# An attention layer and a quantised FFN on one core: P @ latents, the output products and the weight loads moved by some steps

## The chip, the core and the metric

The kernel runs on one core of a Trainium2 chip. The core has TensorE (PE; its weight loads are a row of their own, PEld), VectorE (DVE), ScalarE (ACT), GpSimd (POOL) and SyncE (SP), which issues all transfers of this kernel, one after the other. Each engine works its instructions off in the order of the program and waits for the others by semaphores. The metric is the device time of one launch in microseconds.

## The reference

The input has 8 sequences ("batches") of 512 tokens with 512 features, all in float32. The layer is attention with compressed keys and values, 16 heads, and then a gated FFN whose weights are rounded to 8-bit floats:

```
x = x + attention(layernorm(x))
x = x + ffn(layernorm(x))

attention:  q = rmsnorm(h @ wq_a.T) @ wq_b.T            16 heads, 128 + 64 rotary
            kv_c, k_pe = split(h @ wkv_a.T)             128 latents + 64 rotary
            k, v = split(rmsnorm(kv_c) @ wkv_b.T)       per head
            attn = softmax((q.k + rope(q_pe).rope(k_pe)) / sqrt(192))
            out = (attn @ v) @ wo.T
ffn:        silu(h @ fp8(gate) * gs) * (h @ fp8(up) * us) @ fp8(down) * ds
```

## The kernel before

The weights of a head are folded: `wq_b` with the key half of `wkv_b` into `wa`, the value half of `wkv_b` with `wo` into `wst`. So a head's scores are taken against the 128 latents themselves, and P @ V becomes P @ latents with the value weights applied later.

The attention part is a list of 512 steps, one for each batch, head and tile of 128 queries (`steps`). A step number is `at(b, h, t) = (b * 16 + h) * 4 + t`; within a batch the steps run from 0 to 63, four a head. Each step does the following (`scores`, L547 to L569, and the loop at L793 on):

- First the `rest` of the step before: on VectorE the reciprocal of the row sums (L566), the scaling of the row (L567) and a transpose by blocks of 32 (L167). After every second tile `send` (L172) has SyncE write the block to DRAM (`way`, L177) and read it back, four transfers, as the transposed probabilities `prT` (L179). The second needs the first to have landed.
- Then the scores of this step: TensorE (L555, L557), the row maximum on VectorE (L559, `nmax`), the exponential on ScalarE (L562).
- Then whatever was put into this step of `work`, in the order in which it was put there. `put(i, f)` is all the planning that there is: the numbers in these calls are written by hand, and the order of each engine follows from them, because the scheduler is set to take the program's own order.

What is put there, with the step in the batch at which head h's or group g's work stands (i is the last step of a group's last head, 16 g + 15):

- `project(b, h)` (L537): query projection to the latents, on TensorE, copied out by ScalarE as `qn`. Step 4 h - 3.
- `project_pe`: rotary part for two heads: `qpe` on TensorE, `rotate` on VectorE with a sum on GpSimd (`roped`, L414), `hi` on ScalarE, `lo` on VectorE.
- `attend(b, h)` (L572): P @ latents, eight matmuls (`av`), copied out as `o` by ScalarE. Step 4 h + 8, five steps behind the head's last scores.
- `sums` (L587): four additions on GpSimd over two heads' `o`.
- `output(b, g)` (L601): four heads' contribution to the output, as a product of 2 x 2 blocks with seven products in place of eight. `product` (L616) runs 4 matmuls for a block and then adds the sum in PSUM to a quarter of `x` (L627). The products share sums: four of them go into `u_ps`, one behind the other without clearing, and are read after each; `z_ps` and `v_ps` share a second buffer. So a product into `u` can begin only when VectorE has read `u` for the product before. Steps i + 7, 8, 12 and 15.
- `load_wst`, `load_x`: loads by SyncE of the folded weights and of the batch's input. The buffer of the input, `x`, takes the sum of the attention and is stored to DRAM (`x2`, L631) at the end of the batch, before the next batch's input is loaded into it.
- `round_piece` (L383): in batches 1 to 6, one piece of FFN weights every four steps: load (`raw`), `first` (two operations on VectorE and two on GpSimd, L71 to L77), `rest` (two on VectorE, L81 and L82), store (`done`).
- The next batch's latents, in pieces spread over the batch (`latents`): layer norm, transposes, projection with `wlr` (`project_x`), `norms` (a square root on ScalarE, which changes its function table and back), `scale` (L473, L476), `transpose_l` (L483, L484, TensorE) and `rotary`.

PSUM has six buffers for everything but the products (`ps_r`), taken in turn. The last batch has no latents to make; it loads FFN weights instead. The FFN follows, batch by batch.

Of the kernel before, what the change touches and what calls it, by code (L numbers as in the profile page):

```python
# [43 lines left out]
P = 128  # L44
# [42 lines left out]
class Layer:  # L87
# [182 lines left out]
    def attention(self):  # L270
        tc, nc, ins, wp, xp = self.tc, self.nc, self.ins, self.wp, self.xp
        with ExitStack() as ctx:
# [110 lines left out]
            def round_piece(w, i, half):  # L383

                n = self.size[w]
                cols = slice(half * H // 2, (half + 1) * H // 2)
                got = {}

                def load():
                    got["raw"] = fp.tile([P, H // 2], F32, tag="wo", name="raw")  # L390
                    nc.sync.dma_start(got["raw"], ins[w][i][:, cols])

                def first():
                    got["done"] = fp.tile([P, H // 2], F32R, tag="wo", name="done")
                    got["rest"] = round_e4m3fn(nc, got["done"], got["raw"], sp)

                def store():
                    nc.sync.dma_start(
                        self.scratch[w, i // n][:, i % n, cols].bitcast(F32), got["done"].bitcast(F32)
                    )  # L400

                return load, first, lambda: got["rest"](), store
# [184 lines left out]
            def sums(b, h):  # L587

                even, odd = (state["o", b, h - 1 + k].rearrange("p (u s) -> p u s", u=2) for k in range(2))
                s = hp.tile([P, 3, S // 2], F32, tag="sums", name="sums", bufs=2)
                s2, s3, s4 = (s[:, k, :] for k in range(3))
                nc.gpsimd.tensor_tensor(s3, even[:, 0], even[:, 1], ALU.subtract)
                nc.gpsimd.tensor_tensor(even[:, 1], even[:, 1], odd[:, 1], ALU.add)
                nc.gpsimd.tensor_tensor(s2, even[:, 1], even[:, 0], ALU.subtract)
                nc.gpsimd.tensor_tensor(s4, odd[:, 0], s2, ALU.subtract)
                del state["pe", b, h // 2]
                state["sums", b, h] = even[:, 0], even[:, 1], s2, s3, s4, odd[:, 0], odd[:, 1]

            def output(b, g):  # L601


                x = xs[b]
                ops = [state.pop(("sums", b, g * G + k)) for k in (1, 3)]
                for j in range(G):
                    del state["o", b, g * G + j]
                w = wst_s.pop((b, g))
                c11, c12, c21, c22 = (
                    x[:, 2 * t : 2 * t + 2, k * (H // 2) : (k + 1) * (H // 2)] for t in range(2) for k in range(2)  # L610
                )
                A11, S1, S2, S3, S4, A12, A22 = range(7)
                B11, B21, B22, T1, T2, T3, T4 = range(7)
                got = {}

                def product(name, left, right, c, last=True):  # L616
                    first = name not in got
                    if first:
                        tag = "u" if name == "u" else "v"
                        got[name] = ps_o.tile([P, 2, H // 2], F32, tag=tag, name=f"{name}_ps")  # L620
                    for t in range(2):
                        for p in range(2):
                            nc.tensor.matmul(  # L623
                                got[name][:, t, :], ops[p][left][:, t * P : (t + 1) * P], w[:, p, right, :],
                                start=first and t == 0 and p == 0, stop=last and t == 1 and p == 1, skip_group_check=True,
                            )
                    nc.vector.tensor_tensor(c, c, got[name], ALU.add)  # L627

                def store(t):
                    if g == NG - 1:  # L630
                        nc.sync.dma_start(self.x2[b][:, t : t + 2, :], x[:, t : t + 2, :])  # L631

                return [
                    lambda: (product("u", A11, B11, c11, False), product("z", A12, B21, c11)),
                    lambda: (product("u", S2, T2, c12, False), product("v", S1, T1, c22, False)),
                    lambda: (product("u", S3, T3, c22, False), product("v", S4, B22, c12)),
                    lambda: store(0),
                    lambda: product("u", A22, T4, c21),
                    lambda: store(2),
                ]  # L640
# [14 lines left out]
            def put_q(b, h):  # L655

                i = at(b, h)
                if h % 2 == 0:

                    def rotary_part():  # L660
                        for k, f in enumerate(project_pe(b, h // 2)):
                            put(i - 5 + k, f)

                    put(i - 6, rotary_part)
                put(i - 3, project, b, h)


            p0, state["latents", 0] = latents(0)
# [26 lines left out]


            for b, h in ((b, h) for b in range(B) for h in range(NH)):
                put(at(b, h, 3) + 5, attend, b, h)
            for b, h in ((b, h) for b in range(B) for h in range(NH)):
                if b or h:  # L700
                    put_q(b, h)
            for b, h in ((b, h) for b in range(B) for h in range(1, NH, 2)):
                i = at(b, h, 3)
                put(i + 6, sums, b, h)
                if h % G == G - 1:

                    def projected(b=b, g=h // G, i=i):

                        when = (7, 8, 18, 13, 19, 17) if (b, g) == (B - 1, NG - 2) else (7, 8, 12, 13, 15, 17)
                        for n, f in zip(when, output(b, g)):  # L710
                            put(i + n, f)

                    put(i + 6, projected)

            for h in range(NH):
                if h >= 2:
# [15 lines left out]
            for b in range(1, B):  # L732
                for g in range(NG):
                    for k, f in enumerate(load_wst(b, g)):
                        put(at(b, G * g + 3, 3) - 6 + 2 * k, f)
                for k, f in enumerate(load_x(xs, b, hidden(b), xp, "x")):
                    put(at(b, 4, 1) + k + k // 2, f)

            todo = [(w, i) for i in range(NI) for w in ("wg", "wu")] + [("wd", i) for i in range(NI)]
            for k, (w, i, half) in enumerate((w, i, half) for w, i in todo for half in range(2)):  # L740
                b, n = divmod(k, 12)
                for d, f in zip((-2, 0, 3, 4), round_piece(w, i, half)):
                    put(at(b + 1, n + 2, 1) + d, f)


# [8 lines left out]
            def put_latents(b):  # L754
# [6 lines left out]
                put(at(b - 1, 13), p["norms"])  # L761
                put(at(b - 1, 13, 1), p["norms_inverse"])
                for t in range(NT):
                    put(at(b - 1, 13, 1) + t // 2, p["scale"], t)
                    put(at(b - 1, 13, 3) + t // 2, p["transpose_l"], t)
                put(at(b - 1, 14, 1), p["rotary"])

            def put_ffn():
                stats, apply, transpose, self.y = self.ffn_normed(self.fx[0], sp, ps_r, hp)
# [10 lines left out]
                put(at(b - 1, 3), *((put_latents, b) if b < B else (put_ffn,)))  # L780
            for g in range(NG):
                put(at(B - 1, G * g + 3, 1), self.load_ffn, "wg", g, wp, f"wa{g}")
            put(at(B - 1, NH - 1, 3) + 3, self.load_ffn, "wu", 0, wp, "wst", 2)

            self.gates = {}
            put(
# [3 lines left out]

            with tc.manual_schedule():
                prT = block = rest = None
                for i in range(len(steps) + 18):  # L793
                    if rest:
                        rest()
                        rest = None
# [142 lines left out]
```

## Time and profile before

| | before |
|---|---|
| median of 3 runs | 2803.2 us (2802.39 to 2813.38) |
| the profiled execution | 2801.86 us |
| its span, first to last instruction | 2800.0 us |
| TensorE busy | 2728.4 us, 97% of the span |
| VectorE busy | 1887.1 us, 67% |
| ScalarE, GpSimd busy | 899.0 us, 604.1 us |
| scores of all 512 steps end | 2236.4 us after the span's start |
| one batch in the middle | about 277 us |

The page of a profile lists busy time by engine, the chain of work that ended last, and groups of instructions by line with the idle time of their engine just ahead of them. The timeline gives single instructions: start, duration, engine, line, operation, output and inputs, shape, how often in a row, and in brackets the engine's idle time before it and what ended it. Matmuls overlap, and their ends are modelled, so one of 512 columns is shown as 0.6 us and the next begins after 0.43; an fp32 matmul counts as two instructions. The granted clock of TensorE is a share of full speed.

### The profile page before, as it was taken

The numbers are of one execution on the slowest core, as the hardware profiler recorded it, in microseconds if no ns is written. First come the engines' busy times: TensorE is split into PE (matmuls) and PEld (weight loads), VectorE is DVE, ScalarE is ACT, GpSimd is POOL, SyncE is SP. The second block draws the span as 40 slices with busy tenths as digits, with TensorE's granted clock in tenths as the row PEclk, the third lists the DMA queues.
The fourth block names the chain that finished last, engine by engine and source line by source line (L and its number), as shares of the span: only waits on it lengthen the run. The fifth ranks groups of instructions, "written<-read, shape, count | busy, mean of one in ns | idle before, by whom it ended". The sixth has DMA issues, their size and how long they took to land.

```text
span 2800.0 us, 29251 instructions
## 1 busy us (share of the span) xinstructions
PE 2728.4 (97%) x9264; PEld 1717.8 (61%) x9264; DVE 1887.1 (67%) x3680; ACT 899.0 (32%) x1956; POOL 604.1 (22%) x629
## 2 busy tenths in 40 slices
PE   7999999999999999999999999999999999999999
PEld 4555555555555555555555555555555578888887
DVE  5766777777777777777777777777766733443332
ACT  3333333333333333333333333333232323322222
POOL 1222222212221222122212221222111122222222
PEclk9999999999999999999999999999999999999999
DMA  4654555455545554555455445654565552111110
GB/s 131 211 175 158 170 193 166 154 174 188 169 153 178 184 162 154 178 190 162 152 179 192 159 153 180 194 167 145 176 193 168 178 184 81 61 61 64 64 64 19
DMA packets 262377, 426.07 MB, mean 152 GB/s; under 512 B 29648, under 2 KB 192592, under 8 KB 260688
## 3 DMA queue, kind: packets, MB, share of 16 engines
q1 hardware_dynamic: 262224, 424.21, 47.0%
q8 instruction: 74, 1.21, 0.2%
q14 instruction: 79, 0.65, 0.1%
HBM read 248.99 MB, written 175.11 MB: 151 GB/s over the span
## 4 chain that ended last, share of the span: by engine, by line
PE 85%; DVE 7%; DMA 4%; SPq 1%; issue 1%; ACT 1%; POOL 0%; ACTq 0%; POOLq 0%; DVEq 0%
PE av L578 13%; PE sc L555 13%; PE qn_ps L543 10%; PE u_ps L623 7%; PE sc L557 7%; PE pu L261 6%; PE pd L864 6%; PE pg L261 6%; PE qpe_ps L511 5%; PE lr_ps L448 4%; PE v_ps L623 4%; DMA way<-block 2%; PE z_ps L623 2%; DVE pr L567 2%; DVE block L167 1%; DMA raw<-in_wu 1%
## 5 line engine op out<-in xcount | busy, mean ns | idle before, releaser
L562 ACT ACTIVATE pr<-sc,nmax 128x512 f32<-128x512 f32 x512 | 352.0, 687 | 1296.2 <-DVE nmax L559 1296.0
L557 PE MATMUL sc<-kpe,qpe 128*128 128x512 f32 x1024 | 525.8, 594 | 2.1 <-DVE qpe L531 2.1
L555 PE MATMUL sc<-lat,qn 128*128 128x512 f32 x1024 | 523.1, 592 | 0.0
L578 PE MATMUL av<-prT,kvt 128*128 128x512 f32 x1024 | 471.1, 603 | 28.9 <-DMA prT<-way 19.7
L559 DVE TENSOR_REDUCE nmax<-sc 128x1 f32<-128x512 f32 x512 | 339.0, 662 | 123.2 <-PE sc L557 123.0
L167 DVE STREAM_TRANSPOSE block<-pr 128x512 f32<-128x512 f32 x512 | 364.2, 711 | 21.9 <-DMA way<-block 4.2
L543 PE MATMUL qn_ps<-lat,wa 128*128 128x512 f32 x768 | 350.4, 592 | 0.0
L567 DVE TENSOR_SCALAR pr<-pr,rden 128x512 f32<-128x512 f32 x512 | 334.3, 653 | 18.0
L557 PEld LDWEIGHTS sc<-kpe,qpe 128*128 128x128 f32 x1024 | 194.4, 190 | 247.4 <-issue 242.3
L578 PEld LDWEIGHTS av<-prT,kvt 128*128 128x128 f32 x1024 | 196.2, 193 | 234.6 <-issue 215.0
L414 POOL TENSOR_TENSOR roped<-rope_own,rope_sw 128x512 f32<-128x512 f32 x72 | 91.4, 1270 | 995.2 <-DVE rden L566 896.4
L555 PEld LDWEIGHTS sc<-lat,qn 128*128 128x128 f32 x1024 | 188.9, 190 | 136.1 <-issue 114.3
L543 PEld LDWEIGHTS qn_ps<-lat,wa 128*128 128x128 f32 x768 | 145.3, 189 | 134.5 <-issue 123.0
L852 POOL TENSOR_TENSOR fl<-fuse,fh 128x512 fp32r<-128x512 f32 x96 | 126.6, 1319 | 382.1 <-ACT fh L851 382.1
L848 DVE SCALAR_TENSOR_TENSOR fuse<-pu,us,gate 128x512 f32<-128x512 f32 x96 | 72.0, 750 | 198.3 <-PE pu L261 194.8
L566 DVE RECIPROCAL rden<-den 128x1 f32<-128x1 f32 x512 | 81.6, 159 | 152.3 <-ACT pr L562 144.8
L76 POOL TENSOR_TENSOR q_r<-raw,q_m 128x256 f32<-128x256 f32 x72 | 67.5, 938 | 512.3 <-DVE q_m L74 512.3
L511 PE MATMUL qpe_ps<-lat,wqp 128*128 128x512 f32 x384 | 175.1, 592 | 0.0
L623 PE MATMUL u_ps<-wst,sums 128*128 128x256 f32 x512 | 126.3, 391 | 24.2 <-DVE x L627 16.2
L261 PE MATMUL pg<-yh,wg 128*128 128x512 f32 x384 | 149.6, 390 | 0.0
L261 PE MATMUL pu<-yh,wu 128*128 128x512 f32 x384 | 149.6, 390 | 0.0
L261 PE MATMUL pu<-yl,wu 128*128 128x512 f32 x384 | 149.4, 389 | 0.0
(115 smaller groups left out, 3719.3 us busy)
## 6 DMA issues: line engine op xcount, KB each, us to landing
way<-block SPq DMA_DIRECT2D x256, 512.0 KB, 2.9
prT<-way SPq DMA_DIRECT2D x1024, 128.0 KB, 2.8
wst<-wst_d SPq DMA_DIRECT2D x56, 512.0 KB, 4.4
wst<-wst_d SPq DMA_DIRECT2D x56, 384.0 KB, 3.9
x<-in_hid SPq DMA_DIRECT2D x60, 256.0 KB, 3.4
x<-x SPq DMA_DIRECT2D x16, 512.0 KB, 3.9
out<-o SPq DMA_DIRECT2D x32, 256.0 KB, 2.0
wst_d<-wst SPq DMA_DIRECT2D x8, 896.0 KB, 4.6
```

The source lines that it names most:

```text
L167: self.nc.vector.transpose(out[:, :, :, i : i + Q].rearrange("p c k i -> p k c i"), x.rearrange("p (k c j) -> p k c j", c=NQ, j=Q),)
L261: self.nc.tensor.matmul(ps, self.ffn_w[name, i][:, c * P : (c + 1) * P], y[k][:, c, :], start=c == 0 and k == 0, stop=c == NC - 1 and k == 1,)
L511: nc.tensor.matmul(ps, wqp_s[g][:, r, pj * P : (pj + 1) * P], lat[:, r, :], start=r == 0, stop=r == NR - 1)
L543: nc.tensor.matmul(ps, wa_s[g][:, j, r, :], lat[:, r, :], start=r == 0, stop=r == NR - 1)
L555: nc.tensor.matmul(sc, qn[:, q], lat[:, NR, :], start=True, stop=False)
L557: nc.tensor.matmul(sc, qpe[:, h % 2, q], kpe[:, part, :], start=False, stop=part == 1)
L559: nc.vector.tensor_reduce(nmax, sc, AX.X, ALU.max, negate=True)
L562: nc.scalar.activation(pr, sc, AF.Exp, bias=nmax, accum_out=den)
L567: nc.vector.tensor_scalar(pr, pr, rden, None, ALU.mult)
L578: nc.tensor.matmul(av, kvt[:, kt, :], prT[:, :, :, kt, :], start=kt == 0, stop=kt == NT - 1)
L623: nc.tensor.matmul(got[name][:, t, :], ops[p][left][:, t * P : (t + 1) * P], w[:, p, right, :], start=first and t == 0 and p == 0, stop=la ...
L864: nc.tensor.matmul(pd, f[:, i, t * P : (t + 1) * P], w["wd", i], start=i == 0 and f is fh, stop=i == NI - 1 and f is fl,)
```

## The change

Seven kinds of edit, all of them in when a piece of work stands, none in what it computes:

- `attend` stands six steps behind the head's last scores instead of five; `project` four steps ahead of its head instead of three.
- `sums` moves from 6 to 7 steps behind i, and the products from 7, 8, 12, 15 to 8, 12, 15, 16, the stores of x from 13 and 17 to 16 and 18. In the last batch but one group, whose late steps were 18 and 19 (7, 8, 18, 13, 19, 17), they are 8, 12, 17, 18, 19, 20. The `sums` tile gets a third buffer.
- In the first two pairs of products the one into the other buffer (z, v) now stands first and the one into `u` second.
- `raw` is loaded five steps ahead of `first` in place of two, `rest` follows after one step in place of three, and the store after two in place of four. `raw` uses the buffers of `wqn` and no longer shares those of `done`.
- The input `x` of a batch is loaded in steps 20, 21, 22, 23 in place of 17, 18, 20, 21.
- `scale` of tiles 0 and 1 moves from step 53 to 54, of tiles 2 and 3 from 54 to 56; `transpose_l` of tiles 0 and 1 stays in 55, of tiles 2 and 3 moves from 56 to 57; `rotary` from 57 to 58.
- The loop has one step more at its end, and one FFN load at the end stands one step later.

```diff
-                    got["raw"] = fp.tile([P, H // 2], F32, tag="wo", name="raw")
+                    got["raw"] = fp.tile([P, H // 2], F32, tag="wqn", name="raw")
...
-                s = hp.tile([P, 3, S // 2], F32, tag="sums", name="sums", bufs=2)
+                s = hp.tile([P, 3, S // 2], F32, tag="sums", name="sums", bufs=3)
...
-                    lambda: (product("u", A11, B11, c11, False), product("z", A12, B21, c11)),
-                    lambda: (product("u", S2, T2, c12, False), product("v", S1, T1, c22, False)),
+                    lambda: (product("z", A12, B21, c11), product("u", A11, B11, c11, False)),
+                    lambda: (product("v", S1, T1, c22, False), product("u", S2, T2, c12, False)),
...
-                put(i - 3, project, b, h)
+                put(i - 4, project, b, h)
...
-                put(at(b, h, 3) + 5, attend, b, h)
+                put(at(b, h, 3) + 6, attend, b, h)
...
-                put(i + 6, sums, b, h)
+                put(i + 7, sums, b, h)
...
-                        when = (7, 8, 18, 13, 19, 17) if (b, g) == (B - 1, NG - 2) else (7, 8, 12, 13, 15, 17)
+                        late = (b, g) == (B - 1, NG - 2)
+                        when = (8, 12, 17, 18, 19, 20) if late else (8, 12, 15, 16, 16, 18)
...
-                    put(i + 6, projected)
+                    put(i + 7, projected)
...
-                    put(at(b, 4, 1) + k + k // 2, f)
+                    put(at(b, 5) + k, f)
...
-                for d, f in zip((-2, 0, 3, 4), round_piece(w, i, half)):
+                for d, f in zip((-5, 0, 1, 2), round_piece(w, i, half)):
...
-                    put(at(b - 1, 13, 1) + t // 2, p["scale"], t)
-                    put(at(b - 1, 13, 3) + t // 2, p["transpose_l"], t)
-                put(at(b - 1, 14, 1), p["rotary"])
+                    put(at(b - 1, 13, 2) + t // 2 * 2, p["scale"], t)
+                    put(at(b - 1, 13, 3) + t // 2 * 2, p["transpose_l"], t)
+                put(at(b - 1, 14, 2), p["rotary"])
...
-            put(at(B - 1, NH - 1, 3) + 3, self.load_ffn, "wu", 0, wp, "wst", 2)
+            put(at(B - 1, NH - 1, 3) + 4, self.load_ffn, "wu", 0, wp, "wst", 2)
...
-                for i in range(len(steps) + 18):
+                for i in range(len(steps) + 19):
```

## The prediction

> **What bounds the kernel now.** I read the page's shares first, then its chain, then who waits on TensorE, then the timeline of the places where it waits.
>
> ```profile
> PE 2728.4 (97%) x9264; PEld 1717.8 (61%) x9264; DVE 1887.1 (67%) x3680; ACT 899.0 (32%) x1956; POOL 604.1 (22%) x629
> PE 85%; DVE 7%; DMA 4%; SPq 1%; issue 1%; ACT 1%; POOL 0%; ACTq 0%; POOLq 0%; DVEq 0%
> ```
>
> TensorE (PE) sets the time; only its waits can be won. The view of the waits has few with PE as the waiter: `av` for `prT`, and `u_ps` for VectorE's (DVE's) add. I count steps inside a batch, 0 to 63 (four a head), and take the time from the end of one step's scores to the end of the next, less the ordinary time of that step's matmuls. Ordinary are: scores 1.32 us, `attend` 3.43, `project` and `qpe` 2.58 each, one product 1.72, a tile's transposes 0.44. What is lost by this count, us:
>
> - Batch 0: step 9 0.5, step 17 4.7 (`av` waits for `prT`): 5.2.
> - Batches 1 to 6, each: (a) step 20, `av` for `prT`, 1.6 to 2.4, sum 11.8; (b) step 23, `u_ps` for the add L627, 2.6 to 6.1, sum 23.7; (c) step 55, the same behind the transposes, 1.55, sum 9.4. Together 44.9, or 7.5 a batch.
> - Batch 7: steps 20 and 36, `av`, 6.8 and 4.6: 11.4. Between step 51 and the end of the last `av`, some 13.
>
> Place (b), TensorE and VectorE:
>
> ```profile
> 410.94 1.89 PE L623 MATMUL u_ps<-wst,o 128*128 128x256 f32 x8
> 412.67 1.89 PE L623 MATMUL z_ps<-wst,o 128*128 128x256 f32 x8
> 412.80 0.29 DVE L71 TENSOR_SCALAR q_m<-raw 128x256 uint32<-128x256 uint32 x1 [1.49 <-DMA raw<-in_wu]
> ...
> 417.39 0.67 DVE L627 TENSOR_TENSOR x<-x,u_ps 128x512 f32<-128x512 f32 x1
> 418.21 1.97 PE L623 MATMUL u_ps<-wst,sums 128*128 128x256 f32 x8 [2.33 <-DVE x L627]
> ```
>
> `u_ps` is one sum to which three products are added between reads, so the next `u` product waits for DVE's read. DVE is late (its lag, here and below, is the start of a step's `nmax` after the end of its scores; 5.7 at step 22): it idled for `raw` twice (0.98, 1.49) and for the table loads at step 18.
>
> **What the Trainium skill says.** "TensorE: Matmul & The Clock Gate", Part 1: after an idle window of some 3.4 us the clock halves until a busy one has passed, and the windows run free. The trace agrees: where TensorE waited 2.9 us and more the granted clock mostly fell for 3.4 or 6.8 us. The (b) of batch 1 waited 2.33 and kept full clock; that of batch 3 waited 2.91 and lost 6.1, at a mean granted clock of 0.62 (the column before the last two, of the view by windows):
>
> ```profile
> 968.00:977.00 9.00, 6.59 (x17) 5.31 (x18) 5.46 (x10) 1.56 (x4) 0.07 (x1) 0.62 0.74 236
> ```
>
>  "SBUF — State Buffer", SBUF: two separate sides: VectorE's two-port or two-input operations and a GpSimd operation exclude each other. The trace agrees: L567 takes 0.49 us alone and 1.58 beside GpSimd's 1.27 `roped`; the scale L473 0.41 and 0.89. "ScalarE: Activation LUTs", What ACT_TABLE_LOAD costs: 1283 ns; 1.28 here.
>
> **The change part by part.** No arithmetic is added; TensorE's matmul time is unchanged. The run-ahead of TensorE is bounded by the six buffers that scores share with the projections, some three steps; no lag below exceeds 5 us, so that no wait is costed for them.
>
> *P @ latents, and project.* `project` moves one step forward and `attend` one back, so one `project` (2.58) and one scores (1.3) come between the transfer and its reader, 3.9 us. A product pair between them adds more in steps 14 to 20. All `av` waits of (a) are under 2.4: gone. In step 17 of batch 0, 4.7 is 2.9 of wait and 1.8 of halved clock: gone, as is step 9. Batch 7: 5.1 and 2.9 of wait against 3.9 plus 1.7: gone with their clock. On ACT only the copies of `qn` and `o` change places. The SyncE (SP) queue keeps the order send, loads, send; the x loads now stand three steps behind the x2 store that they wait for (SP waited 22.5 us for it, 7 times), and `raw` and `done` trade places in it. Their buffers were released two pieces before. Gain: 5.2 + 11.8 + 11.4.
>
> *Products.* `u` after `u` one step apart is now the third and fourth time (15, 16) instead of the first and second. Group 0 and 1 have `project_x` (3.88) between them, so (b) goes: 23.7. In group 2 (steps 62, 63) DVE is 2.6 late at its `nmax`: 0.6 + 0.7 puts the read at 3.9, and TensorE wants it at 4.6: no wait. In group 3 (steps 14, 15) DVE is late by 3.1: step 11 takes 8.33 (two adds and the rotation, lag 3.6 at step 12), steps 12 and 13 take 2.91 and 5.24 against 3.89 and 4.76 of TensorE. Then `nmax` 0.6, the `rest` that now stands there 0.84, the add 0.7: read at 5.3 against 4.6. About 0.8 a batch with a blocked operation: +4.8 in six. Nothing queues behind it but the next scores.
>
> *Loads of weights.* `raw` five steps ahead takes DVE's waits (11.8 + 5.7 in all, off the path by themselves) away; `rest` only one step behind `first` has GpSimd's two sums (1.5 to 2.3 us) in front of it and more DVE work than that between: nothing.
>
> *The latents of the next batch, steps 51 to 57.* Here a wait arises. Before:
>
> ```profile
> 826.59 0.65 DVE L559 TENSOR_REDUCE nmax<-sc 128x1 f32<-128x512 f32 x1
> ...
> 831.31 0.89 DVE L473 TENSOR_SCALAR x<-x,rms 128x384 f32<-128x384 f32 x1
> ...
> 832.79 0.69 ACT L562 ACTIVATE pr<-sc,nmax 128x512 f32<-128x512 f32 x1
> ...
> 836.24 0.49 PE L483 MATMUL lat_pt<-ident,x 128*128 128x128 f32 x3
> ...
> 838.60 1.97 PE L623 MATMUL u_ps<-wst,sums 128*128 128x256 f32 x8 [1.33 <-issue]
> ```
>
> The scales stand in step 53 (831.31), five us ahead of the transposes, with the two products of step 54 (3.44) between. After, scales 0 and 1 stand in step 54, which holds nothing for TensorE but its scores, and the transposes in step 55. On the same clock: scores of step 52 end at 822.96, step 53 (`project` 2.58 + 1.3) at 826.85, step 54 (`attend` 3.43 + 1.32) at 831.61, step 55 at 832.93; TensorE wants the first transpose at 832.8. DVE: the exp of step 53 still comes out of ACT's two table loads (norms and back to exp) and is done at 833.57; then reciprocal, norm, transpose 1.36 to 834.95, `nmax` 0.6, `rest` 0.84, scale 0.41: 836.85. So TensorE waits 4.1, and for the later parts 0.3 more: 4.4. GpSimd's four `sums` (0.73 to 0.91 each), released at 834.2, lie beside just these operations; blocked in turn they make it 6.1. I take 5.2. A wait of this length halves the clock for one window or two: 1.6 to 3.1 lost, I take 2.2. Sum 7.4 in place of (c). Behind the transposes TensorE has queued z and u of the group and the scores of step 56; DVE waits for all three, and is on time again after them, so nothing more follows. Six batches: +44.4, and (c) −9.4. In batch 0 `fold_o` (0.86) and a smaller lag leave 1.7 to 2.1 of wait, 2.5 in all: +2.5. In batch 7 there are none. Transposes 2 and 3 at step 57: their copies come 0.3 before the `qpe` of step 58 asks: nothing, up to 1 a batch if not.
>
> *End.* DVE enters step 51 of batch 7 without its old lag of 2.2, and the last transfers follow: −2.8. The last four pairs of products run without scores between, u after u back to back once: +0.9; steps 30/31 and 46/47 of batch 7 +0.4.
>
> Sum: −5.2 −11.8 −11.4 −23.7 −9.4 −2.8 + 4.8 + 44.4 + 2.5 + 1.3 = −11.3. Against the profiled execution (span 2800.0, 2801.9 with what lies around): 2790.6; the median shown is 1.3 above that: about 2792. I round to 2790.
>
> **The rivals.**
> *The new wait stays small.* If DVE is some 3 us earlier at step 54, because ACT's table loads overlap more than in the row above, the wait is 1 to 2 and the clock holds: 1.5 for 7.4, −35: 2755 (2745 to 2775). For it: `hi` and the norms are free of DVE. Against: exp at 832.79 waits for ACT itself, in every batch alike.
> *Slower: the wait at the transposes takes all.* Place: step 55 of batches 1 to 6. Each scale blocked behind a GpSimd sum and two slow windows is 6.1 + 3.4, and the second tile's wait falls into the slow clock. From 9.3 a batch on, (5.2+11.4+2.8−2.5−1.3)/6 + 7.5 − 0.8, the change costs time; at 11.5 it is 6 x 2.2 = 13 above the kernel before, 2816. For it: `sums` moved into this step. Against: L81 and L82 never ran longer than 0.43.
> *P @ latents still waits,* because the transfer itself moves back with DVE: (a) and batch 7 unchanged, 2813. Against: 3.9 us of TensorE work come between whatever DVE does.
>
> **How the numbers follow.** As worked 0.60 (2777 to 2803), small wait 0.20, slower 0.15 (2800 to 2828), transfer 0.05. The measurement tells about 0.5%, 14 us, from no change: below 2789 is faster. As worked gives 0.28 faster and 0.32 same; the small wait all faster; the slower two 0.09 same and 0.11 slower. Faster 0.48, same 0.41, slower 0.11. The range leaves half of the small wait and half of the slower ones out: 2760 to 2812; as worked alone 2777 to 2803.
>
> **What would show it.** TensorE's waits for `prT` gone except at the end; no wait of `u_ps` in step 23; a wait of under 1.2 us of `u_ps` in step 15 of six batches; a wait of 4 to 6 us before `lat_pt` L483 in six batches, with DVE's scale as its end and a dip of the clock; no waits of `q_m` for `raw`. Wrong: no wait before the transposes, or `av` waits left in mid-batch.

## The result, and the profile after

The changed kernel takes 2796.63 us (median of 20 runs, 2792.57 to 2801.54), the kernel before 2801.56 us (20 runs, 2796.36 to 2813.38; the three runs that the forecast had to go by had a median of 2803.2). The ratio is 0.998, with a 95% interval of 0.9971 to 0.9989: some 5 us less, under the 14 us that the forecast called a difference. Forecast were 2790 us, 13 us less than those three runs; 4.9 us less were measured, under half of it. The profiled execution of the changed kernel took 2792.89 us (span 2791.1), 9 us less than that of before.

First part and chain of the page after; the columns are as before.

```profile
PE 2725.8 (98%) x9264; PEld 1720.1 (62%) x9264; DVE 1883.9 (67%) x3680; ACT 898.1 (32%) x1956; POOL 597.8 (21%) x629
...
PE 86%; DVE 8%; ACT 2%; DMA 2%; issue 1%; SPq 0%; POOL 0%; ACTq 0%; DVEq 0%; POOLq 0%
```

TensorE's busy time is nearly the same (2725.8 for 2728.4), so it still sets the time, and only its waits have moved. Who waits for whom on TensorE, after (total, times, longest):

```profile
PE lat_pt L483 <- DVE x L473: 28.1, 8, 4.3
PE av L578 <- DMA prT<-way: 10.5, 2, 10.1
PE u_ps L623 <- DVE x L627: 5.9, 8, 0.8
```

The same view of before:

```profile
PE av L578 <- DMA prT<-way: 19.7, 8, 5.1
PE u_ps L623 <- DVE x L627: 16.2, 6, 2.9
```

Now one wait of 10.1 us for `prT` makes up nearly all of that line (it is the last `av` of all), `u_ps` waits eight times for at most 0.8, and 28.1 us stand at the transposes of the next batch's latents, where the view of before has no wait for VectorE's scale of `x`.

Place (b) of batch 1, timeline of TensorE:

```profile
408.01 3.60 PE L578 MATMUL av<-prT,kvt 128*128 128x512 f32 x8
...
414.10 1.89 PE L623 MATMUL z_ps<-wst,o 128*128 128x256 f32 x8
...
415.83 1.89 PE L623 MATMUL u_ps<-wst,o 128*128 128x256 f32 x8
```

`av` begins without a wait, and so do both products, z first. There is one product into `u` here, in step 23; the one before it stands in step 15, the next in step 27.

Steps 53 to 56 of batch 1, timeline of TensorE, VectorE, ScalarE and GpSimd:

```profile
555.38 1.03 PE L557 MATMUL sc<-kpe,qpe 128*128 128x512 f32 x2
...
556.20 0.69 ACT L562 ACTIVATE pr<-sc,nmax 128x512 f32<-128x512 f32 x1
...
559.20 0.79 POOL L597 TENSOR_TENSOR sums<-o,sums 128x256 f32<-128x256 f32 x1
559.44 0.83 DVE L82 SCALAR_TENSOR_TENSOR done<-q_m,q_r 128x256 fp32r<-128x256 f32 x1
...
560.19 0.41 DVE L473 TENSOR_SCALAR x<-x,rms 128x384 f32<-128x384 f32 x1
...
560.75 0.87 PE L483 MATMUL lat_pt<-ident,x 128*128 128x128 f32 x3 [4.34 <-DVE x L473]
...
562.48 2.65 PE L623 MATMUL z_ps<-wst,o 128*128 128x256 f32 x8
```

The last scores end at 556.4; the exponential of step 53 comes out of the two table loads only at 556.9; then VectorE does the row's scaling and transpose, `nmax`, the two operations of `rest`, and the scale at 560.19. TensorE waits 4.34 us for it by the modelled ends. Counted from the point at which the next matmul could have begun, 0.16 us before the modelled end of the last, it is 4.50 us; most waits below are counted so. `nmax` is at 558.37, L81 takes 0.46; L82, which takes 0.43 alone, takes 0.83 beside GpSimd's `sums`. The first product behind the transposes takes 2.65 in place of 1.89: the granted clock is at half for a stretch, a "dip". By windows (the column before the last two is the granted clock):

```profile
556.00:568.00 12.00, 7.66 (x30) 6.13 (x29) 8.39 (x19) 3.96 (x10) 3.40 (x5) 0.86 0.32 99
```

Of these 12 us TensorE is idle for 4.3, at a mean granted clock of 0.86. This stands in each of batches 1 to 6, with the same 4.50 us and one dip of 3.4 us: from the scores of step 55 to those of 56 it takes 11.8 us where the matmuls take 5.66.

### The profile page after: what moved, and what is told of

Read it like the earlier page. It is cut to its first block, busy times and chain, and to the rows that moved or that the text cites. A ratio compares the mean times of both kernels' runs of the same rounds, so it can differ in the third digit from the quotient of the medians.

```text
span 2791.1 us, 29188 instructions
## 1 busy us (share of the span) xinstructions
PE 2725.8 (98%) x9264; PEld 1720.1 (62%) x9264; DVE 1883.9 (67%) x3680; ACT 898.1 (32%) x1956; POOL 597.8 (21%) x629
## 4 chain that ended last, share of the span: by engine, by line
PE 86%; DVE 8%; ACT 2%; DMA 2%; issue 1%; SPq 0%; POOL 0%; ACTq 0%; DVEq 0%; POOLq 0%
PE av L578 13%; PE sc L555 13%; PE qn_ps L543 10%; PE u_ps L623 7%; PE sc L557 7%; PE pu L261 6%; PE pd L865 6%; PE pg L261 6%; PE qpe_ps L511 6%; PE lr_ps L448 4%; PE v_ps L623 3%; PE z_ps L623 2%; DMA way<-block 2%; DVE pr L567 2%; DVE nmax L559 1%; DVE block L167 1%
## 5 line engine op out<-in xcount | busy, mean ns | idle before, releaser
L578 PE MATMUL av<-prT,kvt 128*128 128x512 f32 x1024 | 462.5, 594 | 13.1 <-DMA prT<-way 10.5
L261 PE MATMUL pg<-yl,wg 128*128 128x512 f32 x384 | 149.4, 389 | 0.0
```

What stands on the lines that cost most here:

```text
L261: self.nc.tensor.matmul(ps, self.ffn_w[name, i][:, c * P : (c + 1) * P], y[k][:, c, :], start=c == 0 and k == 0, stop=c == NC - 1 and k == 1,)
L578: nc.tensor.matmul(av, kvt[:, kt, :], prT[:, :, :, kt, :], start=kt == 0, stop=kt == NT - 1)
```

## Experiments on the changed kernel: the transposes, the start and the end

The theory T: (a), (b) and (c) are gone, and their gain is given back at the transposes of step 55, where VectorE's scale is late. The rival R1: VectorE is late there anyway, and the wait only changes its place. The second theory, T2, is for the two terms of the sum that the trace contradicts, the start and the end.

**e1: the scales alone put back.**

```diff
-                    put(at(b - 1, 13, 2) + t // 2 * 2, p["scale"], t)
+                    put(at(b - 1, 13, 1) + t // 2, p["scale"], t)
```

> The changed kernel with one thing undone: the scales of the next batch's latents stand again in steps 53 and 54 (they were moved to 54 and 56). Theory T (what the change wins is given back in step 55 of batches 1 to 6, where TensorE waits 4.5 us before the transposes for VectorE's scale and then runs 3.4 us or more at half clock): the wait before lat_pt is under 0.5 us in all six batches, step 55 falls from 11.8 to about 5.7, and the time falls by 6 x 6.1 + 2.5 = 39 us or a little more, since repeated launches may have had longer dips of the clock than the profiled one: about 2756 (2748 to 2764). Rival R1 (VectorE is late there whatever the order, and the wait passes to the next reader, the products behind the transposes or the second pair of transposes): a wait of 2 us or more remains in steps 55 to 58, and the time stays above 2775.

Measured: 2764.42 us (2761.54 to 2765.61), ratio to before 0.986 (0.9843 to 0.9877), 32 us less than the changed kernel of e4, on the same chip. The wait before `lat_pt` is gone in all six batches and step 55 takes 5.73. The time is 8 us above the middle of what T expected and 0.4 above its range, and the trace has those 8 us in one place (timeline of batch 1):

```profile
555.61 0.49 PE L483 MATMUL lat_pt<-ident,x 128*128 128x128 f32 x3
...
571.02 1.08 ACT L485 COPY lat<-lat_pt 128x512 f32<-128x512 f32 x2
...
572.15 2.84 PE L511 MATMUL qpe_ps<-lat,wqp 128*128 128x512 f32 x6 [1.13 <-ACT lat L485]
```

TensorE now arrives at `qpe` on time and finds ScalarE's copies of the transposes of step 57, which the change moved there, 1.13 us late (1.3 by the ends of the steps), in each of six batches. So T holds, and R1 for a small part: 1.3 of the 6.1 us pass to the next reader. In the changed kernel, where TensorE comes 4.5 us later, nothing waits there.

**e2: the first pair of products back in step 54.**

```diff
-                        when = (8, 12, 17, 18, 19, 20) if late else (8, 12, 15, 16, 16, 18)
+                        when = (8, 12, 17, 18, 19, 20) if late else (7, 12, 15, 16, 16, 18)
```

> The changed kernel with only the first pair of products 7 instead of 8 steps behind the group, so that step 54 has 3.44 us of TensorE work again between its scores and the transposes; the scales stay where the change put them. T: VectorE's scale is as late as before, and the products cover 3.4 of the 4.5 us: the wait before lat_pt falls to about 1.1 us (0.6 to 1.7), no dip of the clock follows, and the time falls by 6 x 5 = 30 us, to about 2766 (2758 to 2775). Rival R1 (the scale falls behind whatever TensorE does, as the two adds to x now stand near it): the wait stays above 3 us, and the time within 5 us of the changed kernel's.

Measured: 2773.95 us (2771.80 to 2775.97), ratio 0.9897 (0.9882 to 0.9913), 23 us less than the changed kernel. The wait before `lat_pt` went altogether, but not as expected: the products themselves wait (timeline, batch 1).

```profile
556.36 0.58 ACT L581 COPY o<-av 128x512 f32<-128x512 f32 x1
...
556.99 2.67 PE L623 MATMUL z_ps<-wst,o 128*128 128x256 f32 x6 [1.99 <-ACT o L581]
...
559.68 0.41 DVE L473 TENSOR_SCALAR x<-x,rms 128x384 f32<-128x384 f32 x1
```

`o` of the group's last head is copied by ScalarE behind the exponential of step 53, since `attend` now stands one step later; z waits 2.16 us for it. That wait and the products together pass 4.5 us, so the transposes find their scale. The cover was worth what T said, but in this order it has a wait of its own.

**e3: the large transfers at both ends elsewhere.**

```diff
-                        put(at(b, G * g + 3, 3) - 6 + 2 * k, f)
+                        put(at(b, G * g + 3, 3) - (14 if (b, g) == (B - 1, NG - 1) else 6) + 2 * k, f)
...
+                late = 0 if b else 6
...
-                    put(i, moments, t)
-                put(at(b, 4, 2), deviation)
-                put(at(b, 4, 3), deviation_inverse)
+                    put(i + late, moments, t)
+                put(at(b, 4, 2) + late, deviation)
+                put(at(b, 4, 3) + late, deviation_inverse)
...
-                    put(at(b - 1, 0, 1) + 2 * k, f)
+                    put(at(b - 1, 0, 1) + (2 * k if b > 1 else 11 + k), f)
...
-                put(at(B - 1, G * g + 3, 1), self.load_ffn, "wg", g, wp, f"wa{g}")
+                put(at(B - 1, G * g + 3, 1) + (4 if g == NG - 1 else 0), self.load_ffn, "wg", g, wp, f"wa{g}")
```

> The changed kernel with three sets of transfers elsewhere. Start: the next batch's input is loaded in steps 12 to 15 of batch 0 instead of 1, 3, 5, 7, its statistics six steps later. End: the last piece of wg is loaded behind the last blocks of probabilities instead of between them, and the last four pieces of wst eight steps earlier. Theory T2 (the two terms of the forecast that failed, start and end, are set by SyncE's queue: a block that is sent behind a large load lands late, whatever TensorE and VectorE do): the wait before the last av falls from 10 us to 2 to 5, the end gains 5 to 9 us; the wait for prT in step 17 of batch 0 (2.5) goes, 1 to 4 us; in all 2786 (2782 to 2791). Rival R2 (VectorE's lag or the chain write, land, read itself sets the end, not the loads between): the wait before the last av stays over 8 us, and the time within 2 us of the changed kernel's.

Measured: 2786.25 us (2781.38 to 2787.74), ratio 0.9938 (0.9922 to 0.9955), 10.5 us less than the changed kernel: T2. SyncE's queue at the end, of the changed kernel and then of e3 (one issue a line, `prT` four):

```profile
2227.48 0.43 SPq L129 DMA_DIRECT2D wg<-wgd  x1
...
2228.01 0.38 SPq L177 DMA_DIRECT2D way<-block  x1
...
2236.41 1.75 SPq L179 DMA_DIRECT2D prT<-way  x4
...
2238.72 0.38 SPq L177 DMA_DIRECT2D way<-block  x1
...
2244.72 1.74 SPq L179 DMA_DIRECT2D prT<-way  x4
```

```profile
2231.16 0.34 SPq L177 DMA_DIRECT2D way<-block  x1
...
2233.79 1.73 SPq L179 DMA_DIRECT2D prT<-way  x4
```

A block is written (L177), and read back (L179) when it has landed. Behind 384 KB of `wst` and 768 KB of `wg` this took 8.4 us, behind 512 KB of `wst` 6.0, with neither 2.6 to 2.9. TensorE's wait before the last `av` fell from 10.24 to 1.23 us. From the end of step 51's scores to the end of the last `av` before had 67.3 us, the changed kernel 66.3, e3 55.3. At the start the wait of 2.5 us went, 1.5 us appeared in front of a later `av` of batch 0, and from its first scores to step 54 it took 231.9 us for 234.1. The loads of `wg` and of `wst` moved together, so that their shares of the gain at the end aren't known apart.

**e4: the changed kernel again.**

> The changed kernel itself, for a second profile on the chip of these runs. T: 2796.6 again, and in step 55 of batches 1 to 6 the same wait of 4.5 us; each is followed by one or two dips of the clock of 3.4 us, and how many there are makes the difference between launches (2792.6 to 2801.5): a launch at a granted clock of 0.991 or 0.992 has three to five more dips than the profiled one at 0.994. Rival R3: the number of dips is the same and the differences come from the transfers at the start and the end.

Measured: 2796.74 us (12 runs, 2793.43 to 2798.95), ratio 0.9982 (0.9973 to 0.9991). The waits of its profile are those of the first, to 0.02 us (4.50 six times); the dips are not: two of the six lasted 6.8 us in place of 3.4. Timeline and windows of such a batch:

```profile
562.07 3.62 PE L623 MATMUL z_ps<-wst,o 128*128 128x256 f32 x8
...
565.48 2.21 PE L623 MATMUL u_ps<-wst,o 128*128 128x256 f32 x8
```

```profile
555.00:570.00 15.00, 10.67 (x35) 7.88 (x34) 10.08 (x22) 4.55 (x10) 3.99 (x5) 0.77 0.28 87
```

The first product now runs at half clock throughout and the second in part, and this batch loses 7.3 us in place of 6.1; the other with a long dip loses 6.8. Over the 32 launches of the changed kernel, of these runs and the first, time follows the mean granted clock: 2792.8 us at 0.994 (2 launches), 2794.5 at 0.993 (5), 2796.6 at 0.992 (17), 2799.2 at 0.991 (7), 2801.3 at 0.990 (1). The profiled execution was one of the two at 0.994. This favours T over R3: the same waits with longer dips behind them. That the dips of the other launches lie at these waits is inferred; only two launches were profiled.

## Experiments on the kernel before: each edit alone

**e5: only the products.** The order z, u and v, u, the steps 8, 12, 15, 16, the stores of `x`, its load in steps 20 to 23, the third `sums` buffer, the loop's end and the FFN load at the end; as in the diff of the change, nothing else of it.

> The kernel before with only the products moved: 8, 12, 15, 16 steps behind the group, z and v first, the stores, the load of x, the third sums buffer and the loop's end with them. T: (b), the wait of u_ps in step 23 (23.7 us in six batches), and (c), the one in step 55 (9.4), go; step 15 gets 0.8 us in each; no wait arises at the transposes, since the scales still stand in step 53. About 28 us less than before: 2774 (2768 to 2781). Rival R4 (VectorE's lag is only carried on to the next product that adds to u): waits of u_ps of over 2 us remain in six batches, and the time stays above 2787.

Measured: 2753.26 us (2751.39 to 2754.26), ratio 0.9823 (0.9807 to 0.9838): 48 us less than before, 20 more than T had. (b) and (c) are gone, and so are the waits of `av` in mid-batch from batch 1 to step 51 of batch 7 (one of 0.4 us is left in batch 4), though `attend` stands where it stood. Timeline of batch 1, steps 17 to 20, first one line of before and then e5:

```profile
402.21 3.67 PE L578 MATMUL av<-prT,kvt 128*128 128x512 f32 x8 [1.65 <-DMA prT<-way]
```

```profile
395.56 0.69 DVE L559 TENSOR_REDUCE nmax<-sc 128x1 f32<-128x512 f32 x1
...
398.24 1.75 SPq L179 DMA_DIRECT2D prT<-way  x4
...
404.47 3.60 PE L578 MATMUL av<-prT,kvt 128*128 128x512 f32 x8
```

VectorE takes `nmax` of step 17 at once (lag 0.04; before 3.6), `prT` is issued at 398.24 (before: 397.93), and TensorE comes for it at 404.5 instead of 400.6. The transfer is no earlier; its reader is later. Which part of this edit removes (b), the new steps or the order with `z` and `v` first, was not tried.

**e6: only P @ latents and project.**

```diff
-                put(i - 3, project, b, h)
+                put(i - 4, project, b, h)
...
-                put(at(b, h, 3) + 5, attend, b, h)
+                put(at(b, h, 3) + 6, attend, b, h)
...
-                put(i + 6, sums, b, h)
+                put(i + 7, sums, b, h)
...
-                    put(i + 6, projected)
+                    put(i + 7, projected)
```

`sums` has three buffers here too. The products are not moved, although what was expected of this run takes them to be: the last line of the edit moves the planning of the products, not their numbers, and the trace has them in steps 22, 23, 27 and 30 as before. So they now stand right behind the later copies and sums that they read.

> The kernel before with only P @ latents six steps behind its scores, project four steps ahead, and sums and products one step later with it (8, 9, 13, 16; u after u still one step apart, third sums buffer). T: the waits of av in mid-batch, (a) 11.8 and batch 7's 11.4, go, the start gains nothing; (b) stays or grows where VectorE gets less time before it: 2780 (2774 to 2790). Rival R5 (what is won at (a) is lost at (b), because TensorE arrives there earlier and VectorE does not): only batch 7's 11 us are won, 2791 or more.

Measured: 2807.38 us (13 runs, 2799.36 to 2813.82), ratio 1.0019 (1.0008 to 1.0029): slightly slower than before, where T had a gain of 20 us. Who waits on TensorE:

```profile
PE u_ps L623 <- DVE x L627: 19.9, 9, 3.7
PE z_ps L623 <- ACT o L581: 7.3, 12, 2.2
...
PE u_ps L623 <- POOL sums L596: 4.6, 1, 4.6
```

(a) and the waits of batch 7 are gone but for one of 0.9 us, as the forecast said (11.8 and 11.4 us). But the waits for VectorE's add are larger than before (19.9 for 16.2), z waits for the copy of `o`, and one product of batch 0 waits 4.6 us for GpSimd's `sums`. By the steps, batches 1 to 6 lose 15.4 us in steps 22 and 23, more than (a) gives; batch 7 keeps 7.6 us of its gain up to step 51; batch 0 loses 7.8 up to step 54, nearly all at the wait for `sums` and the dip behind it. For batches 1 to 6 that is what R5 says. How much of the loss comes from TensorE's earlier arrival, and how much from the products having stayed where they were, this run can't tell apart.

**e7: only the loads of weights.**

```diff
-                    got["raw"] = fp.tile([P, H // 2], F32, tag="wo", name="raw")
+                    got["raw"] = fp.tile([P, H // 2], F32, tag="wqn", name="raw")
...
-                for d, f in zip((-2, 0, 3, 4), round_piece(w, i, half)):
+                for d, f in zip((-5, 0, 1, 2), round_piece(w, i, half)):
```

> The kernel before with only the weights to be rounded loaded five steps ahead, rest one and store two steps behind. T: VectorE's waits for raw (0.98 and 1.49 us ahead of place (b)) go, so that (b) shrinks by up to 2.5 us a batch, while rest now stands closer to it: 2794 (2788 to 2801). Rival R6: nothing within 3 us, since VectorE is bound there by its own work.

Measured: 2805.25 us (20 runs, 2799.43 to 2809.66), ratio 1.0011 (1.0003 to 1.0019). VectorE's waits for `raw` went, and the loss at (b) fell from 23.7 to 4.7 us over the six batches, more than T had. The gain went elsewhere: 10.2 us more are lost in step 55, where `rest` now stands in step 54 ahead of it ((c) costs 2.4 us, or 4.1 with a dip, for 1.55), 3.0 in step 20, 3.6 in step 39 and 4.4 in steps 0 and 4. In the profiled executions the six batches took 1663.1 us for 1661.0. So R6 is near in the time, 3 to 4 us more than before, but not in its reason: (b) did depend on when the weights are loaded and finished.

**e8: only the latents.**

```diff
-                    put(at(b - 1, 13, 1) + t // 2, p["scale"], t)
-                    put(at(b - 1, 13, 3) + t // 2, p["transpose_l"], t)
-                put(at(b - 1, 14, 1), p["rotary"])
+                    put(at(b - 1, 13, 2) + t // 2 * 2, p["scale"], t)
+                    put(at(b - 1, 13, 3) + t // 2 * 2, p["transpose_l"], t)
+                put(at(b - 1, 14, 2), p["rotary"])
```

> The kernel before with only the scales, transposes and rotary part of the next batch's latents moved (scales 54 and 56, transposes 55 and 57, rotary 58). Products of 3.44 us still stand in step 54. T: the scale is as late as in the changed kernel, but the products cover it, so that the wait before lat_pt is 0.5 to 1.5 us and (c), 1.55, mostly goes; the time stays within 5 us of before: 2801. Rival R1 (the scale is late whatever covers it): 3 us or more of wait in six batches, and 2815 or more.

Measured: 2797.30 us (15 runs, 2793.75 to 2804.29), ratio 0.9984 (0.9975 to 0.9993). No wait before `lat_pt` in batches 1 to 6, and (c) is down to 0.4. The late scale costs nothing as long as two products stand ahead of the transposes.

## Experiments on what goes together

These four ran on a chip on which the kernel before took 2796.36 us, 5 less than on the others; so a difference to e5 is given both by times and by ratios.

**e9: the changed kernel without the latents' move** (the diff of e8 undone).

> The changed kernel with the whole move of the next batch's latents undone (scales 53 and 54, transposes 55 and 56, rotary 57): the products, P @ latents and the loads moved. T: neither the wait before the transposes nor the one of 1.3 us before qpe in step 58, which appeared when only the scales were put back, is there: 2764.4 less 6 x 1.3, 2756 (2750 to 2761), a little above the products alone (2753.3), because the waits of the start and the end are longer. Rival R7 (P @ latents and the loads cost several us by themselves in the middle of the batches): 2763 or more.

Measured: 2754.90 us (2754.21 to 2755.84), ratio 0.985 (0.9837 to 0.9864). Neither the wait at the transposes nor the one at `qpe` is there; in batches 1 to 6 some 1.1 us a batch are left, nearly all of it `u_ps` in step 15. T; by its ratio it would be about 2759 us on a chip like that of e5, which is still inside T's range. Against e5 P @ latents and the loads win nothing: 1.6 us more by times, 0.27% by ratios, with intervals that just touch; the wait at the end is 2 us longer (9.2 for 7.3).

**e10: before with products and latents moved** (the diffs of e5 and e8).

> The kernel before with the products moved and the latents moved, nothing else. T (each of the two edits alone costs nothing, together they do: one takes the products out of step 54, the other puts the scale there): a wait of 4 to 5 us before lat_pt in six batches, with dips of the clock, 6.1 to 7.4 us each, and 2.5 in batch 0: 2753.3 plus 39 to 47, about 2795 (2788 to 2801). Rival R8 (the wait needs the move of P @ latents too, whose copy stands on ScalarE beside the exponential of step 53): waits under 2 us and less than 2770.

Measured: 2782.39 us (2779.40 to 2783.80), ratio 0.9947 (0.9933 to 0.9960); the latents' move, worth 4 us of gain in e8, costs 29 us by times and 1.2% by ratios here.

```profile
558.24 0.52 PE L483 MATMUL lat_pt<-ident,x 128*128 128x128 f32 x3 [3.23 <-DVE x L473]
```

The wait is 3.39 us in all six batches, with a dip in five. It is the same wait as in the changed kernel, 1.1 us shorter: there `rest`, L81 and L82 with 0.46 and 0.83, stands in step 54 in front of the scale; here, with the loads not moved, it does not. R8 falls; T's 4 to 5 was too high, and so was its time.

**e11: e5 with the last group's pairs early.**

```diff
-                        when = (8, 12, 17, 18, 19, 20) if late else (8, 12, 15, 16, 16, 18)
+                        when = (8, 12, 17, 18, 19, 20) if late else (8, 9, 12, 13, 16, 18) if g == NG - 1 else (8, 12, 15, 16, 16, 18)
```

> The kernel of e5 (only the products moved) with the pairs of the last group of a batch at 8, 9 and 12 instead of 8, 12 and 15, so that they stand in steps 7, 8 and 11 of the next batch, where VectorE is on time, and not in 7, 11 and 14; the other groups as in e5, the stores of x at 13 and 18. T3 (the waits (a) of av in step 20 went because a pair of products, 3.44 us of TensorE for 1.33 of VectorE, was moved into the stretch in which VectorE is behind): VectorE's lag at step 17 is 3.5 us again and av waits 1.4 to 2.4 us in step 20 of six batches, 2753.3 plus 6 x 1.9, about 2764 (2760 to 2769). Rival R9 ((a) came from SyncE's wait for the x2 store ahead of the load of x, which the products' edit also moved): no wait in step 20, 2750 to 2757.

Measured: 2760.22 us (2758.28 to 2760.70), ratio 0.9868 (0.9854 to 0.9881), above e5 by 7 us in times and by 0.45% in ratios. VectorE's lag at step 17 is 3.98 us, and `av` waits again in step 20 of each batch: 0.9 to 1.9 us in batches 1 to 6 (1.36 in the mean, where T3 had 1.9), 3.95 and a dip in batch 7. Timeline of batch 1:

```profile
397.30 1.75 SPq L179 DMA_DIRECT2D prT<-way  x4
...
401.59 3.67 PE L578 MATMUL av<-prT,kvt 128*128 128x512 f32 x8 [1.09 <-DMA prT<-way]
```

The loads of `x` and its last store are as in e5, and its first store is three steps earlier than there, so R9, which would have no wait here, falls. T3: with the rest as in e5, where this pair of products stands decides whether (a) is there.

**e12: e5 with the ends of e3 and the last product one step later.**

```diff
-                        when = (8, 12, 17, 18, 19, 20) if late else (8, 12, 15, 16, 16, 18)
+                        when = (8, 12, 17, 18, 19, 20) if late else (8, 12, 15, 16, 17, 19)
```

> The kernel of e5 with the transfers of start and end moved as in e3 and the last product at 17 (store at 19). T: the wait before the last av falls from 7.3 to 1 to 3 us, the one in step 17 of batch 0 (3.3 and a dip) goes, and those of 0.7 us of u_ps in step 15 go: 2753.3 less 6, 3 and 4, about 2741 (2736 to 2747). Rival: the last product in step 16 of the next batch brings a new wait of its own, 2748 or more.

Measured: 2741.93 us (2736.58 to 2744.15), ratio 0.9797 (0.9784 to 0.981): the fastest of all, 2.0% below the kernel before; its interval and that of e5 (0.9807 to 0.9838) just touch. By windows, batches 1 to 6 (end of the last scores of batch 0 to that of batch 6), the kernel before, the changed one, and this:

```profile
324.26:1984.42 1660.16, 1625.59 (x5113) 948.09 (x5113) 1284.96 (x2532) 541.53 (x1249) 363.38 (x399) 1.00 0.54 171
```

```profile
326.95:1985.60 1658.65, 1627.91 (x5113) 952.26 (x5113) 1283.06 (x2532) 540.85 (x1248) 361.40 (x398) 0.99 0.54 172
```

```profile
327.04:1943.90 1616.86, 1616.31 (x5114) 944.41 (x5113) 1282.49 (x2532) 540.32 (x1248) 363.89 (x399) 1.00 0.54 176
```

The first number is the stretch, the second TensorE's busy time in it. Before, 34.6 us of the six batches were idle; the changed kernel has 30.7; here 0.5 are left, at full clock. At the start T missed: three waits of `av` of 1.2 to 2.5 us in batch 0, one with a dip, are left there.

## Where the prediction was wrong, and what in it held

The sum, stage by stage on the profiled executions (predicted, measured, us):

| stage | predicted | measured |
|---|---|---|
| up to step 54 of batch 0 | −5.2 | −0.1 |
| batch 0, step 55 | +2.5 | +2.8 |
| batches 1 to 6 | +4.3 | −1.5 |
| batch 7 up to step 51 | −11.0 | −9.7 |
| end of attention | −1.9 | +0.6 |
| FFN | 0 | −1.0 |
| sum | −11.3 | −8.9 |

**What held.** The bound; (a), (b), (c) and batch 7's waits gone in mid-batch; 0.95 us of `u_ps` in step 15 for 0.8; the wait at the transposes in step 55 of six batches, ended by VectorE's scale, 4.5 us for "4.4 to 6.1, I take 5.2", with a dip each time. With a dip of 3.4 us a batch loses 6.1, with one of 6.8 us it loses 7.3 or 6.8 (e4); the forecast's 7.4 was the upper end, and six batches came out 6 us better than the sum in the profiled execution. Batch 0's 2.5 was 2.8.

**The steps that failed.** Two terms of the sum, both gains, were mis-sized by about all that they were; most of the remaining miss of the medians lies in the spread between launches. First, the start, "P @ latents ... as is step 9: gone", −5.2: mis-sized by all of it. The forecast put 3.9 us of TensorE work between the transfer and its reader and took the transfer as fixed. `project` one step earlier stands ahead of the first block that is sent, and the queue of batch 0 is full of loads for the folding: the first block left at 55.42 for 51.83, and the `prT` that the `av` of head 2 waits for was issued at 99.53 for 94.16, 5.4 us later. That eats the 3.9 us: the wait is 2.5 where it was 2.9. The rival that the transfer moves back was dismissed with "whatever DVE does"; it was TensorE's own work and SyncE that moved it. What is won at step 17, 2.1 us with the dip that went, is lost again in this execution: 0.7 to a new wait of `av` in step 25 and 1.7 to a dip at the first scores, which the profile of before doesn't have. In e4's profile, whose dip comes ahead of the first scores, the way from there to step 54 took 232.4 us for 233.8, so that up to 1.5 of the 5.2 may be won in some launches.

Second, the end, "DVE enters step 51 without its old lag ... −2.8": measured nothing gained, +0.6 with the products. VectorE did come to step 51 without its lag (0.36 us for 2.20), but the last transfers did not follow. e3 shows why: the last blocks wait behind `wg` and `wst`, not for VectorE. TensorE came earlier and waited 10.2 us in one place for 3.9 and 3.9 before in two, and the `av` behind it took 5.70 us for 3.60.

Third, launch by launch. These two terms bring −11.3 to −3.3; the better middle and the FFN bring it to −8.9 in the profiled execution. Its launch was one of the two at the highest granted clock; the median lies 3.7 us above it (before: 0.3 below). Two longer dips made e4's six batches 2.1 us longer; that more of them make up the rest is inferred. That leaves −4.9 of the medians. The forecast had allowed for longer dips in the term of 7.4 a batch, and the rounding from 2792 to 2790 made the miss 2 us larger. That six batches came out 6 us better than the sum, as the wait was near its low end, made up for most of the two failed terms in the profiled execution; this was luck.

**Waits that went, and a credit that is too large.** (a) and batch 7's waits, 23 us, were credited to P @ latents. That move is enough to remove them (e6), but e6 wins no time by it; and it isn't needed for it: e5 leaves it out and loses both waits, and with the products moved, it and the loads together win nothing (e9). e11 brings (a) back by moving one pair of products. In steps 9 to 11 VectorE is on time, so a pair of products just ahead of them only lengthens the step for both (e11: step 8). From step 12 on it is behind, and there (e5: step 14) it gains nearly all of the pair's 3.44 us, because its two adds cost it little: its steps 14 to 16 take 9.41 us with them and 9.13 without, and its lag at step 17 is 0.04 for 3.98. The forecast counted moved products as removing a wait on `u_ps`, and did not count that the same TensorE time, put where VectorE lags, removes the waits behind it as well. So of 48 us that the products alone bring, the rest of the change gives 43 back, nearly all of it by the latents' move (without that, e9 has a ratio of 0.985 for 0.998); that the kernel before had that much to give, the forecast's own 44.9 us of lost time plus 11.4 of batch 7 had said.

**The loads.** "Off the path by themselves" does not hold: without VectorE's waits for `raw`, and with `rest` and the store moved, (b) shrank by 19 us in e7. Where the products are moved as well (b) is gone anyway, so that the loads win nothing in the change (e9). And `rest` moved close behind `first` lengthens the new wait from 3.4 us (e10) to 4.5; the forecast had its 0.84 in the chain, and it took 1.3.

**The Trainium skill.** "TensorE: Matmul & The Clock Gate", Part 1, says that the windows run free of the program, and the dips fit that: with a wait of 4.5 us every batch had one, of 3.4 or 6.8 us (12 of 12 in two profiles); with 3.39, five of six; with 2.16 in e2, two of six. It differs in the size: an idle window is some 3.4 us there, and here waits of 2.16 us were at times enough. "SBUF — State Buffer", SBUF: two separate sides, agrees: the forecast's doubt, that L81 and L82 never ran longer than 0.43, fell: L82 took 0.83 beside GpSimd, and in e1 the scale 0.94 for 0.41.

## What to carry to other kernels

When two engines keep step, look for the stretches in which the second one is behind, and move work there that the first needs long and the second short; here this removed the waits behind that place too (e5, e11), while shifting one reader alone (e6) won nothing, because the time was lost at the readers behind it. Two edits that cost nothing alone can cost much together when one is the other's cover: ask of every moved piece what stood ahead of it. And a transfer can be late because of what was issued just before it (8.4 us for 2.6 here): list the queue before taking a landing time as fixed. Last, read from the trace that an edit moved what it was to move, before reading its time (e6).

## What the runs showed of the hardware

The same wait at the same place, to 0.02 us, was followed by a dip of the clock of 3.4 us in one launch and of 6.8 in another; one thousandth of mean granted clock was worth about 2.2 us over 32 launches of some 2796 us. In the e1 profile a wait of 10.65 us before the last `av` brought 13.7 us of half clock. Waits of 2.16 us were followed by a dip in two of six batches, of 3.39 us in five, of 4.50 us in all. A 512 KB write took 2.6 to 2.9 us from its issue to that of the read which waits for it when no load stood just ahead of it in SyncE's queue, 6.0 us behind a load of 512 KB, and 8.4 us half a microsecond behind loads of 384 and 768 KB.
